# Self-attention: row sums of the exponentials taken from ScalarE's accumulator over the first round's scores, with the layer norm's scaling and the squares given to GpSimd

## The chip, the cores and the metric

The kernel runs on one core of one Trainium2 chip. A core has five engines that run their own instruction streams and wait for each other by semaphores: TensorE (PE, matrix products; its weight loads are listed apart as PEld), VectorE (DVE), ScalarE (ACT), GpSimd (POOL) and SyncE (SP, which here only issues transfers). PE writes to PSUM; the other data lies in SBUF. The metric is the device time of one execution in microseconds (us), lower being better.

## The reference, cut to what matters

The program is one decoder layer in float32 over 32 sequences of 128 tokens with 512 features: differential self-attention, cross-attention, and a mixture of experts. The change touches the self-attention alone:

```python
x = x + attn(layernorm(x))
# in attn: 16 heads with two sides each = 32 score maps of head size 16
q = (x @ Wq) * HD**-0.5 ; k = x @ Wk ; v = x @ Wv       # v: 16 heads of size 32
aw = softmax(q @ k.T + causal)                          # for each head and side
aw = aw[side 0] - lam * aw[side 1]
attn = aw @ v
attn = attn * rsqrt(mean(attn * attn, -1) + 1e-5) * (1 - LAMBDA_INIT)
return attn @ Wo
```

## The kernel before, in words

`self_attention` (from L103) works on the 32 sequences in **steps**. A step (b, cp) handles one sequence b and half of its score maps: CP = 2 chunks c of four heads j, each with two sides, so 16 maps of 128 queries by 128 keys. There are 64 steps, two for each sequence, and the loop from L451 is a software pipeline over them: pass n starts step n and does the later parts of the steps before it.

- `normalize` (L180, by `shifted`, L74): h = x*rstd + down, one ScalarE instruction of 128x512 with two per-partition operands. `turn_in` (L186) transposes h on PE (L83) and copies it out (hT, L194).
- `queries_and_keys` (L196): products L207, one pass for each quarter of the features; ScalarE takes keys and queries out of PSUM (kz, L213; qT, L218); GpSimd makes a second form of the keys, k1 (L214), with one added row that carries the maximum. `values` (L220): product L225, copy L229.
- `maxima` (L231), the first round: the scores go to PSUM with queries as rows (L238); VectorE adds the causal mask and writes them to SBUF as `s` (two instructions, L244), then takes each row's negated maximum into the tile `nm` (two instructions, L251).
- `turn_maxima` (L256), one pass later: nm is transposed on PE (L262) and VectorE puts the maxima into the queries, qm (L264).
- `exponentials` (L270), the second round: the scores are computed again, keys as rows and with the maximum already subtracted (L279); ScalarE takes the exponential of all of them (two instructions of 128x1024, L286); GpSimd sets the masked half to zero in place (two instructions, L289).
- `weigh` (L295), two passes after `maxima`: eight products of v with the exponentials (L303), and eight products of a column of ones with the same exponentials (L309), which give the sums of the softmax. Both land in one PSUM tile `po`, in 32x32 blocks; VectorE transposes the blocks, 128x768, into `u` (L314).
- `divide` (L319): reciprocal of the sums (L323), the second side's times -lambda (L324), and o = u times that (L327).
- `finish` (L334), after a sequence's second step: the two sides are added on GpSimd (at, L338), squared on ScalarE (sq, L342), and summed by head on VectorE (ms, L344 and L345); GpSimd takes the power -1/2 (rr, L347). `scale_out` (L350) multiplies on VectorE (an, L353), `turn_out` transposes (anT, L361), `leave` (L369) multiplies by Wo (L374) and adds the residual (xres, L378).

The steps alternate. I call **step A** the pass that ends a sequence's `weigh` (its `divide` is followed by `finish`) and that holds `values` and `turn_in`; **step B** is the other, with `scale_out` (an) at its head and `leave` (xres) at its end. PSUM is handed out by `bank()` (L48) as four buffers of two banks, in turn: who asks for one waits until the tile of four requests ago has been read. The queries and keys of step A (L207) so wait for the tile that `leave` filled, that is for L378.

A scheduler orders each engine's instructions ahead of time; on the chip every engine works through its list in order. VectorE's list around the change is, in step A: qm, anT, s, nm, then u (L314), L323, L324, o (L327), ms, L345, qm; in step B: an (L353), s, a statistic of the next input (L56), nm, L58, L60, u, L323, L324, o, xres. GpSimd's list is, in step A: k1, two selects (L289), at, rr; in step B: k1, two small layer-norm instructions (L62, L66, of which L62 waits for VectorE's L60), two selects. ScalarE's list is, in step A: kz twice, qT, two exponentials, sq, v, hT, h; in step B: kz twice, qT, two exponentials.

After the self-attention come cross-attention, the shared experts and the routed experts.

Of the kernel before, what the change touches and what calls it, by code (L numbers as in the profile page):

```python
# [10 lines left out]
F32 = mybir.dt.float32  # L11
I32 = mybir.dt.int32
AF = mybir.ActivationFunctionType
ALU = mybir.AluOpType
# [4 lines left out]
P = 128  # L19
# [83 lines left out]
def self_attention(cm, x, x1_d, Wq, Wk, Wv, Wo, lq1, lk1, lq2, lk2, heads, heads_in, beside):  # L103
# [14 lines left out]
    nc, tc, bank = cm.nc, cm.tc, cm.banks  # L118
    B = x.shape[0]
    H, D, G = 16, 32, 2  # L120
    CP = 2
    ROW = (16, 0)
    with ExitStack() as ctx:
        wp = ctx.enter_context(tc.tile_pool(name="a_w", bufs=1))
        p1 = ctx.enter_context(tc.tile_pool(name="a_p1", bufs=1))
        p2 = ctx.enter_context(tc.tile_pool(name="a_p2", bufs=2))
# [6 lines left out]
        xin, xres = {}, {}  # L133
# [37 lines left out]
        nc.scalar.activation(begun, cm.mhalf[:, 0:1], AF.Exp)  # L171

        hT, qT, kz, k1, vs = {}, {}, {}, {}, {}
        h, qm, expd, u, o, an = {}, {}, {}, {}, {}, {}

        def measure(b):
            if b < B:
                h[b] = cm.moments(pj2, xin[b], "a_")

        def normalize(b):  # L180
            if b < B:
                rstd, down = h[b]
                h[b] = pj2.tile([P, E], F32, name="h")
                cm.shifted(h[b], xin.pop(b), rstd, down)

        def turn_in(b):  # L186

# [32 lines left out]
        def values(g, i):  # L220
            if g * G >= B:
                return
            pv = bank()[:, 0, :]
            for ec in range(EC):
                nc.tensor.matmul(  # L225
                    pv, hT[g][:, ec, ts(i, P)], w["wv"][:, ec, :], start=ec == 0, stop=ec == EC - 1
                )
            vs[g, i] = p2.tile([P, E], F32, name="v", bufs=3)
            nc.scalar.copy(vs[g, i], pv)  # L229

        def maxima(b, cp):  # L231

            g, i = divmod(b, G)
            sc = [bank() for _ in range(2)]
            for c in range(CP):
                for j in range(4):
                    rows, oc = ts(j, 32), CP * cp + c
                    nc.tensor.matmul(  # L238
                        sc[j // 2][:, j % 2, ts(c, 2 * P)],
                        qT[g][rows, oc, i, :], kz[g, oc][rows, i], start=True, stop=True,  # L240
                    )
            s = p1.tile([P, 4, CP, 2, P], F32, name="s")
            for pair in range(2):
                nc.vector.tensor_tensor(  # L244
                    s[:, 2 * pair : 2 * pair + 2].rearrange("p j c s k -> p (j c s) k"),
                    sc[pair].rearrange("p j (x k) -> p (j x) k", k=P),
                    causal.unsqueeze(1).broadcast_to([P, 4 * CP, P]), ALU.add,
                )
            for side in range(2):
                at = nm[(CP * b + cp) % 2][:, side].rearrange("p (j r) -> p j r", r=32)  # L250
                nc.vector.tensor_reduce(  # L251
                    at[:, :, ROW[side] : ROW[side] + CP], s[:, :, :, side, :], AX.X, ALU.max,
                    negate=True,
                )

        def turn_maxima(b, cp):  # L256

            g, i = divmod(b, G)
            tr = bank()[:, 0, 0 : 2 * P].rearrange("p (s x) -> p s x", s=2)
            qm[b, cp] = p2.tile([P, 2, CP, P], F32, name="qm")  # L260
            for side in range(2):
                nc.tensor.transpose(tr[:, side], nm[(CP * b + cp) % 2][:, side], cm.ident)  # L262
            for side in range(2):
                nc.vector.scalar_tensor_tensor(  # L264
                    qm[b, cp][:, side], qT[g][:, CP * cp : CP * cp + CP, i, :],
                    others[:, side : side + 1],
                    tr[:, side].unsqueeze(1).broadcast_to([P, CP, P]), ALU.mult, ALU.add,
                )
# [26 lines left out]
        def weigh(b, cp):  # L295


            g, i = divmod(b, G)
            po = bank()
            es = [expd.pop((b, cp, pair)) for pair in range(2)]  # L300
            for c in range(CP):
                for j in range(4):
                    nc.tensor.matmul(  # L303
                        po[ts(j, 32), 0, ts(c, 2 * P)], vs[g, i][:, ts(4 * (CP * cp + c) + j, D)],
                        es[j // 2][:, j % 2, c], start=True, stop=True,
                    )
            for c in range(CP):
                for j in range(4):
                    nc.tensor.matmul(  # L309
                        po[ts(j, 32), 1, 0 : 2 * P], ones[:, c, :], es[j // 2][:, j % 2, c],  # L310
                        start=c == 0, stop=c == CP - 1,
                    )
            u[b, cp] = p1.tile([P, 6, 4, D], F32, name="u")
            nc.vector.transpose(  # L314
                u[b, cp].rearrange("p n k d -> p (n k d)"),
                po.rearrange("p two n -> p (two n)")[:, 0 : 6 * P],
            )

        def divide(b, cp):  # L319

            t = u.pop((b, cp))
            rs = p2.tile([P, CP, 2, 4], F32, name="rs")
            nc.vector.reciprocal(rs.rearrange("p c s k -> p s k c"), t[:, 4:6, :, 0:CP])  # L323
            nc.vector.tensor_scalar(rs[:, :, 1, :], rs[:, :, 1, :], nlam, None, ALU.mult)  # L324
            if cp == 0:
                o[b] = p1.tile([P, 2 * CP, 2, 4 * D], F32, name="o")
            nc.vector.tensor_tensor(  # L327
                o[b][:, CP * cp : CP * cp + CP].rearrange("p c s (k d) -> p (c s k) d", d=D),
                t[:, 0:4].rearrange("p n k d -> p (n k) d"),
                rs.rearrange("p c s k -> p (c s k)").unsqueeze(2).broadcast_to([P, 8 * CP, D]),  # L330
                ALU.mult,
            )

        def finish(b):  # L334

            both = o.pop(b)
            at = p1.tile([P, H, D], F32, name="at")
            nc.gpsimd.tensor_tensor(  # L338
                at.rearrange("p (c k) d -> p c (k d)", c=EC), both[:, :, 0], both[:, :, 1], ALU.add
            )  # L340
            sq = p1.tile([P, H, D], F32, name="sq")
            nc.scalar.activation(sq, at, AF.Square)  # L342
            ms = p2.tile([P, H], F32, name="ms")
            nc.vector.tensor_reduce(ms, sq, AX.X, ALU.add)  # L344
            nc.vector.tensor_scalar(ms, ms, 1.0 / D, EPS, ALU.mult, ALU.add)  # L345
            rr = p2.tile([P, H], F32, name="rr")
            nc.gpsimd.tensor_tensor(rr, ms, cm.mhalf, ALU.pow)  # L347
            an[b] = at, rr
# [48 lines left out]
            )  # L397
        nc.vector.tensor_scalar(others, others, -1.0, 1.0, ALU.mult, ALU.add)


        ones = wp.tile([P, CP, D], F32, name="a_ones")
        nc.vector.memset(ones, 0.0)
        for c in range(CP):
            nc.vector.memset(ones[:, c, c : c + 1], 1.0)

        for b in range(G):
            measure(b)

# [9 lines left out]


        nm = [wp.tile([P, 2, P], F32, name=f"a_nm{i}") for i in range(2)]  # L420
        for t in nm:
            nc.gpsimd.memset(t, 0.0)

        for b in range(G):
            normalize(b)
# [25 lines left out]
        for n in range(len(steps) + 5):  # L451
            g, k = divmod(n, 2 * G)
            if n == len(steps) - 2 * G:
                early.close()
            at = {ago: steps[n - ago] for ago in range(6) if 0 <= n - ago < len(steps)}
            if 1 in at:
                turn_maxima(*at[1])
            if 0 in at:
                maxima(*at[0])
            queries_and_keys(g + 1, k)  # L460
            if 1 in at:
                exponentials(*at[1])
            if 2 in at:
                weigh(*at[2])
            if k % 2:
                values(g + 1, k // 2)
            elif 5 in at:
                leave(at[5][0])
            if 3 in at and at[3][1]:
                scale_out(at[3][0])  # L470
            if 2 in at:
                divide(*at[2])
                if at[2][1]:
                    finish(at[2][0])
            b = (g + 2) * G + k // 2
            if k % 2 == 0:
                measure(b)
                if 4 in at:
                    load_again(at[4][0])
            else:  # L480
                normalize(b)
                turn_in(b)
                load(b + G)
                if 4 in at:
                    turn_out(at[4][0])
            if n in beside:
                beside[n]()


class CrossAttention:  # L490
# [19 lines left out]
    ROW = (16, 0)  # L510
# [612 lines left out]
class Shared:  # L1123
# [4 lines left out]
    G = 4  # L1128
# [540 lines left out]
```

## Time and profile before

| | |
|---|---|
| ten runs | median 3960.17 us (3950.39 to 3965.82) |
| profiled execution | 3958.99 us, its span 3957.3 us |
| granted PE clock, whole run | 0.994 |
| self-attention, even stretch | from 107.13 us to 742.15 us, 25 sequences |
| the same stretch, busy | PE 620.79, PEld 396.45, DVE 494.11, ACT 208.33, POOL 282.53 us of 635.02 |
| self-attention's last product L309 | starts at 848.0 us |

Times in the traces count from the span's start. A line of the timeline gives the start, how long the instruction (or a run of equal instructions, with xN) took, the engine, the line of the code, what it writes and reads, and in brackets how long its engine sat idle before it and what ended that. PE's instructions overlap each other, so that PE's busy share is near the whole wherever it has something in its queue, also when it waits inside. An engine that is idle for part of each sequence is not thereby unimportant: what counts is who waits for it last.

### The profile page before, as it was taken

What the parts mean: (1) busy time and instruction counts of PE and PEld (TensorE: products, weight loads), DVE (VectorE), ACT (ScalarE), POOL (GpSimd) and SP (SyncE); (2) the same over time, 40 slices, a digit from 0 to 9 for tenths busy, and PEclk for the clock granted to TensorE, in tenths of its full rate; (3) what the DMA queues carried; (4) which work ended last, traced back from release to release, by engine and by line L of the source; (5) the groups of instructions that cost most, each with busy time, mean ns of one, the idle gap of its engine ahead of it and who ended that gap; (6) DMA issues with size and microseconds to landing.
All of it is one profiled execution on the core that took longest, in us unless ns stands there. A gap on an engine that the chain in (4) does not pass through costs nothing. (4 is left out here: it accounts for less than half of the span.)

```text
span 3957.3 us, 58171 instructions
## 1 busy us (share of the span) xinstructions
PE 3849.3 (97%) x20020; PEld 2026.3 (51%) x20020; DVE 2200.5 (56%) x3525; ACT 1191.7 (30%) x1696; POOL 2255.8 (57%) x2420
## 2 busy tenths in 40 slices
PE   8999999989999999999999999999999999999999
PEld 5666666633433343434445555555555555555444
DVE  5777777778888888888522333333333333333111
ACT  3333333325655556665410111111111111111000
POOL 4444444453666666666325777777777777775000
PEclk9999999989999999999999999999999999999999
DMA  3101110121111111111126778677777777777210
GB/s 109 33 31 30 33 33 28 33 85 34 57 49 60 49 46 49 49 46 44 41 89 161 182 160 195 142 190 164 176 170 165 170 168 171 167 171 160 80 64 32
DMA packets 285980, 387.22 MB, mean 98 GB/s; under 512 B 147888, under 2 KB 179248, under 8 KB 285616
## 3 DMA queue, kind: packets, MB, share of 16 engines
q0 software_dynamic: 62912, 109.85, 15.9%
q1 hardware_dynamic: 81792, 190.98, 15.2%
q10 hardware_dynamic: 140976, 82.60, 7.5%
q8 instruction: 162, 2.65, 0.3%
q14 instruction: 138, 1.13, 0.1%
HBM read 617.52 MB, written 143.07 MB: 192 GB/s over the span
## 5 line engine op out<-in xcount | busy, mean ns | idle before, releaser
L1381 POOL DMA_INDIRECT e_xr<-h_d,e_run_of x832 | 849.4, 1021 | 288.4 <-issue 267.9
L653 DVE TENSOR_REDUCE nm<-ps 128x2 f32<-128x1024 f32 x512 | 610.8, 1219 | 61.6 <-PE ps L649 59.9
L1411 DVE TENSOR_TENSOR e_gu<-e_act,ps 128x352 f32<-128x352 f32 x208 | 108.4, 521 | 930.6 <-ACT e_act L1410 930.6
L676 ACT ACTIVATE xp<-ps 128x1024 f32<-128x1024 f32 x512 | 510.3, 1022 | 282.3 <-PE ps L649 213.7
L1442 PE MATMUL ps<-wd,e_guT 128*128 128x512 f32 (+1 forms) x1248 | 570.1, 592 | 2.0 <-issue 2.0
L672 PE MATMUL ps<-xqn,xk 32*128 32x512 f32 x2048 | 537.8, 623 | 20.2 <-ACT xp L676 19.8
L649 PE MATMUL ps<-xk,xq 32*128 32x512 f32 x2048 | 537.2, 628 | 1.5 <-DVE xres L378 1.4
L1406 PE MATMUL ps<-wg,e_xT 128*128 128x352 f32 x1664 | 528.2, 460 | 4.8 <-DMA wg<-in_L_ffn_w_gate_dram 4.8
L1406 PE MATMUL ps<-wu,e_xT 128*128 128x352 f32 x1664 | 526.6, 459 | 0.9 <-DMA wu<-in_L_ffn_w_up_dram 0.9
L1406 PEld LDWEIGHTS ps<-wg,e_xT 128*128 128x128 f32 x1664 | 315.2, 190 | 239.6 <-issue 104.2
L1406 PEld LDWEIGHTS ps<-wu,e_xT 128*128 128x128 f32 x1664 | 315.8, 190 | 178.4 <-DMA wu<-in_L_ffn_w_up_dram 3.1
L1447 POOL DMA_INDIRECT sum_d<-e_y,e_into x208 | 338.2, 1626 | 117.1 <-issue 69.5
L1442 PEld LDWEIGHTS ps<-wd,e_guT 128*128 128x128 f32 (+1 forms) x1248 | 237.2, 190 | 246.6 <-issue 203.8
L1410 ACT ACTIVATE e_act<-ps 128x352 f32<-128x352 f32 x208 | 96.4, 463 | 886.5 <-PE ps L1406 832.4
L672 PEld LDWEIGHTS ps<-xqn,xk 32*128 32x128 f32 x2048 | 165.2, 183 | 243.2 <-ACT xp L676 101.0
L1446 ACT ACTIVATE e_y<-ps,e_weight 128x512 f32<-128x512 f32 x208 | 142.9, 687 | 422.6 <-PE ps L1442 415.3
L1432 DVE STREAM_TRANSPOSE e_guT<-e_gr 96x384 f32<-96x384 f32 (+1 forms) x416 | 230.4, 554 | 63.9 <-DMA e_gr<-e_gu_d 57.4
L687 PE MATMUL ps<-xp,v 128*32 128x512 f32 x2048 | 246.0, 598 | 8.8 <-ACT xp L676 8.7
L987 POOL DMA_INDIRECT table_d<-entry,at x192 | 196.5, 1023 | 71.8 <-issue 48.0
L1393 DVE STREAM_TRANSPOSE e_xT<-e_xr 128x512 f32<-128x512 f32 x208 | 226.1, 1087 | 11.9 <-DMA e_xr<-h_d,e_run_of 11.9
L214 POOL TENSOR_SCALAR k<-kz,a_keep,a_extra 128x256 f32<-128x256 f32 x128 | 70.0, 556 | 259.0 <-ACT kz L213 259.0
L649 PEld LDWEIGHTS ps<-xk,xq 32*128 32x128 f32 x2048 | 161.2, 183 | 31.0 <-issue 9.4
(267 smaller groups left out, 4956.2 us busy)
## 6 DMA issues: line engine op xcount, KB each, us to landing
wg<-in_L_ffn_w_gate_dram SPq DMA_DIRECT2D x208, 704.0 KB
wu<-in_L_ffn_w_up_dram SPq DMA_DIRECT2D x208, 704.0 KB
wd<-in_L_ffn_w_down_dram SPq DMA_DIRECT2D x208, 576.0 KB
e_gu_d<-e_gu ACTq DMA_DIRECT2D x208, 192.0 KB
e_gr<-e_gu_d ACTq DMA_DIRECT2D x208, 192.0 KB
wd<-in_L_ffn_w_down_dram SPq DMA_DIRECT2D x208, 128.0 KB
e_xr<-h_d,e_run_of POOLq DMA_INDIRECT x832, 3.4
xres<-in_x_dram SPq DMA_DIRECT2D x32, 256.0 KB
```

Of the source, the lines that this page charges most:

```text
L649: self.nc.tensor.matmul(sc[:, i, :], q[rows, ts(c, P)], k[rows, :], start=True, stop=True)
L653: self.nc.vector.tensor_reduce(at[:, self.ROW[side], 2 * pair : 2 * pair + 2], sc, AX.X, ALU.max, negate=True)
L672: self.nc.tensor.matmul(sc[:, i, :], k[rows, ts(c, P)], q[rows, :], start=True, stop=True)
L676: self.nc.scalar.activation(e, sc, AF.Exp)
L687: self.nc.tensor.matmul(po[b, side][ts(j, 32), :], self.v2[b % 2][:, c, 2 * j + side, :], es[j // 2][:, j % 2, :], start=c == 0, stop=c == ...
L987: self.nc.gpsimd.indirect_dma_start(out=self.table_ds[k % 2][:, :], out_offset=bass.IndirectOffsetOnAxis(ap=self.at[b][:, k : k + 1], axis=0),
L1381: self.cm.nc.gpsimd.indirect_dma_start(out=xr[:, t, :], out_offset=None, in_=self.h3_d.rearrange("t (q f) -> (t q) f", q=self.Q), in_offse ...
L1393: self.cm.nc.vector.transpose(xT.rearrange("p c (t i) -> p c t i", t=self.Q), self.xr.pop(i).rearrange("p t (j c) -> p c t j", c=EC),)
L1406: nc.tensor.matmul(pgu[:, half, 0:M], t[:, c, :], w[:, c, :], start=c == 0, stop=c == EC - 1)
L1432: self.cm.nc.vector.transpose(t[rows, 0:n, :].rearrange("p c (t i) -> p c t i", t=self.Q), g[rows, :, 0 : 32 * n].rearrange("p t (j c) -> ...
L1442: nc.tensor.matmul(py, t[:n, c, :], self.wd[s][:n, c, :], start=c == 0, stop=c == len(M_CHUNKS) - 1)
L1447: nc.gpsimd.indirect_dma_start(out=self.sum_d[:, :], out_offset=bass.IndirectOffsetOnAxis(ap=self.into[:, i : i + 1], axis=0), in_=y[:, :] ...
```

## The change

The sums of the softmax come from the first round's scores: `sums` takes the exponential of each of the 16 maps of `s` (128x128) on ScalarE, with the row's negated maximum as bias, and lets ScalarE's accumulator put the row's sum into one column of a new tile `sm`. It works in place on `s`, which therefore has two buffers and not one. In `weigh` the eight products with ones are gone; one PE transpose of `sm` takes their place, `u` has 128x640 elements and not 128x768, and `divide` reads the sums from their new places. Two pieces of ScalarE's work go to GpSimd: the layer norm's scaling from the fifth sequence on, and the squares.

```diff
     def normalize(b):
...
-                cm.shifted(h[b], xin.pop(b), rstd, down)
+                if b < 2 * G:
+                    cm.shifted(h[b], xin.pop(b), rstd, down)
+                else:
+                    nc.gpsimd.tensor_scalar(h[b], xin.pop(b), rstd, down, ALU.mult, ALU.add)
...
-            s = p1.tile([P, 4, CP, 2, P], F32, name="s")
+            s = sc_of[b, cp] = p2.tile([P, 4, CP, 2, P], F32, name="s")
...
+        def sums(b, cp, c):
+            n = (CP * b + cp) % 2
+            s = sc_of[b, cp]
+            for j in range(4):
+                for side in range(2):
+                    at = 32 * j + ROW[side] + c
+                    to = 32 * j + 2 * c + side
+                    nc.scalar.activation(
+                        s[:, j, c, side, :], s[:, j, c, side, :], AF.Exp,
+                        bias=nm[n][:, side, at : at + 1], accum_out=sm[n][:, to : to + 1],
+                    )
...
-            for c in range(CP):
-                for j in range(4):
-                    nc.tensor.matmul(
-                        po[ts(j, 32), 1, 0 : 2 * P], ones[:, c, :], es[j // 2][:, j % 2, c],
-                        start=c == 0, stop=c == CP - 1,
-                    )
-            u[b, cp] = p1.tile([P, 6, 4, D], F32, name="u")
+            nc.tensor.transpose(po[:, 1, 0:P], sm[(CP * b + cp) % 2], cm.ident)
+            u[b, cp] = p1.tile([P, 5, 4, D], F32, name="u")
             nc.vector.transpose(
                 u[b, cp].rearrange("p n k d -> p (n k d)"),
-                po.rearrange("p two n -> p (two n)")[:, 0 : 6 * P],
+                po.rearrange("p two n -> p (two n)")[:, 0 : 5 * P],
             )
...
-            nc.vector.reciprocal(rs.rearrange("p c s k -> p s k c"), t[:, 4:6, :, 0:CP])
+            nc.vector.reciprocal(rs.rearrange("p c s k -> p k (c s)"), t[:, 4, :, 0 : 2 * CP])
...
-            nc.scalar.activation(sq, at, AF.Square)
+            nc.gpsimd.tensor_tensor(sq, at, at, ALU.mult)
...
             if 1 in at:
                 turn_maxima(*at[1])
+                sums(*at[1], 0)
             if 0 in at:
                 maxima(*at[0])
             queries_and_keys(g + 1, k)
             if 1 in at:
                 exponentials(*at[1])
+                sums(*at[1], 1)
```

As the scheduler places it, VectorE's list keeps its order. ScalarE's list is now, in step A: kz twice, qT, two exponentials, nine sums, v, hT, seven sums; in step B: kz twice, qT, two exponentials, sixteen sums. The sixteen sums in step B read the `s` that step A wrote, and the next step A writes into that same buffer; likewise the sums in step A read the `s` of the step B before. GpSimd's list is, in step A: k1, two selects, at, sq, h, rr. From cross-attention on, every engine's list is what it was.

More of the change, by code (lines that the diff above doesn't have):

```diff
@@ L173, in self_attention @@
         hT, qT, kz, k1, vs = {}, {}, {}, {}, {}
-        h, qm, expd, u, o, an = {}, {}, {}, {}, {}, {}
+        h, sc_of, qm, expd, u, o, an = {}, {}, {}, {}, {}, {}, {}
         def measure(b):
@@ L254, in maxima @@
                 )
+        def sums(b, cp, c):
[9 more added lines that the diff above has]
+                    )
+            if c == CP - 1:
+                del sc_of[b, cp]
         def turn_maxima(b, cp):
@@ L398, in self_attention @@
         nc.vector.tensor_scalar(others, others, -1.0, 1.0, ALU.mult, ALU.add)
[L401 to L404, printed above, removed]
         for b in range(G):
@@ L420, in self_attention @@
         nm = [wp.tile([P, 2, P], F32, name=f"a_nm{i}") for i in range(2)]
-        for t in nm:
+        sm = [wp.tile([P, P], F32, name=f"a_sm{i}") for i in range(2)]
+        for t in nm + sm:
             nc.gpsimd.memset(t, 0.0)
```

## The prediction, made before the changed kernel was run

> **What bounds the kernel now.** I read the page first, then the busy times of one stage, then two steps of the timeline, engine by engine. The page points at PE:
>
> ```profile
> PE 3849.3 (97%) x20020; PEld 2026.3 (51%) x20020; DVE 2200.5 (56%) x3525; ACT 1191.7 (30%) x1696; POOL 2255.8 (57%) x2420
> ```
>
> That is a mean over stages. The change touches only self-attention, so here is that stage, 100 us of it:
>
> ```profile
> core 0: us, PE busy (x) PEld busy (x) DVE busy (x) ACT busy (x) POOL busy (x), PEclk, DMA share, GB/s
> 400.00:500.00 100.00, 97.94 (x860) 62.21 (x858) 78.41 (x110) 33.56 (x56) 45.57 (x48) 1.00 0.11 31
> ```
>
> By these shares PE is full, and ScalarE has 66 us in 100 to give away. But the weight loads fill only 62%, so PE's busy time hides waits. The timeline of one sequence (step A from 449.44 us, step B from about 462 us) tells who waits for whom:
>
> ```profile
> 454.36 1.94 ACT L286 ACTIVATE e<-ps 128x1024 f32<-128x1024 f32 x2
> 455.14 1.05 PE L309 MATMUL ps<-e,a_ones 128*32 128x256 f32 x16
> 455.46 2.13 POOL L289 TENSOR_SCALAR_AFFINE_SELECT e<-e 128x1024 f32<-128x1024 f32 x2 [0.53 <-ACT e L286]
> 456.26 0.98 DVE L314 STREAM_TRANSPOSE u<-ps 128x768 f32<-128x768 f32 x1 [0.78 <-PE ps L309]
> 457.57 0.23 DVE L324 TENSOR_SCALAR rs<-rs,nlam 128x8 f32<-128x8 f32 x1
> 457.83 0.69 DVE L327 TENSOR_TENSOR o<-u,rs 128x512 f32<-128x512 f32 x1
> 458.61 1.27 POOL L338 TENSOR_TENSOR at<-o 128x512 f32<-128x512 f32 x1 [1.02 <-DVE o L327]
> 459.91 0.63 ACT L342 ACTIVATE sq<-at 128x512 f32<-128x512 f32 x1 [3.61 <-POOL at L338]
> 460.57 0.69 DVE L344 TENSOR_REDUCE ms<-sq 128x16 f32<-128x512 f32 x1 [2.04 <-ACT sq L342]
> 461.55 2.92 POOL L347 TENSOR_TENSOR rr<-ms,mhalf 128x16 f32<-128x16 f32 x1 [1.67 <-DVE ms L345]
> 464.50 0.69 DVE L353 SCALAR_TENSOR_TENSOR an<-at,rr 128x512 f32<-128x512 f32 x1 [2.26 <-POOL rr L347]
> 465.11 2.35 DVE L244 TENSOR_TENSOR s<-ps,causal 128x1024 f32<-128x1024 f32 x2
> ...
> 467.40 1.94 ACT L286 ACTIVATE e<-ps 128x1024 f32<-128x1024 f32 x2 [0.40 <-PE ps L279]
> 470.43 0.15 DVE L60 TENSOR_SCALAR a_ln_ve<-a_ln_mv 128x1 f32<-128x1 f32 x1
> 471.31 0.26 POOL L66 TENSOR_SCALAR a_ln_down<-a_ln_mv,a_ln_rstd 128x1 f32<-128x1 f32 x1
> 471.52 2.14 POOL L289 TENSOR_SCALAR_AFFINE_SELECT e<-e 128x1024 f32<-128x1024 f32 x2
> 471.80 0.84 DVE L324 TENSOR_SCALAR rs<-rs,nlam 128x8 f32<-128x8 f32 x1
> 472.67 1.53 DVE L327 TENSOR_TENSOR o<-u,rs 128x512 f32<-128x512 f32 x1
> 474.12 0.68 DVE L378 TENSOR_TENSOR xres<-xres,ps 128x512 f32<-128x512 f32 x1
> 474.85 1.59 PEld L207 LDWEIGHTS ps<-hT,wk 128*128 128x128 f32 x8 [0.79 <-DVE xres L378]
> ```
>
> Read it as a loop, each line starting where the one before it ends. PE's L309 ends at 456.19 and u starts. Then o, at, sq, ms, rr, an and s follow with gaps under 0.1 us. In step B the masked scores lead on to xres, and PE's next L207 waits for xres to free its PSUM buffer: the loop closes, 25.36 us after 449.49. Its parts: from xres to u 6.82 us (PE: L207, L279, L303, L309); u to the end of o 2.26; o to s 6.59; s to the end of xres 9.69 (465.11 to 474.80). VectorE alone, without PE's part, is only 0.78 us shorter: that is how long u waits for L309. So a saving counts only on this loop, and PE's share in it is one L309 of the two in a sequence.
>
> One more thing is to be seen: L324 takes 0.84 us in step B and 0.23 in step A; o takes 1.53 and 0.69. In step B two selects run on GpSimd, each 1.09 us (471.52 to 472.61, to 473.66). L324 ends at 472.64, just behind the first; o ends 0.54 us behind the second. These two instructions make no headway while a select runs. In step A the selects end at 457.59, as L324 starts.
>
> **The change part by part,** in the times of this lap.
>
> *L309 out, a transpose in (step A).* L303's last product ends at 455.33 (16 in 1.07 us from 454.26). A PE transpose of 128x128 takes 0.27 us (the L262 rows, weight load 0.14 us); u follows 0.07 us behind as now, so near 455.71: 0.55 us earlier, with bounds of 0.4 and 0.7 for how soon the transpose can start. VectorE is free from 455.48.
>
> *u is smaller.* 768 elements take 0.98 us, 512 (L361) 0.70: one 128 less is 0.14 us less, 0.84. L324 would start at 456.87 and o end at 457.82, 0.70 earlier than now. But the selects still run until 457.59, since they hang on step A's exponentials, which do not move. If L324 waits as in step B, it ends at 457.62 and o at 458.34. **The gain is then 0.18 us and not 0.70.** The Trainium skill ("SBUF — State Buffer", section "Who interferes with whom") states that GpSimd and such a VectorE instruction exclude each other for a whole instruction, whichever starts first; step B's rows show it, no row shows it in step A. By it the lap gains 0.18 here, without it 0.70.
>
> *u in step B* gains nothing: o's end there hangs on the selects, and they on L60, L62 and L66, which stay.
>
> *Squares on GpSimd.* A 128x512 product of two SBUF operands there is L338's row, 1.27 us, for 0.63 plus a hop of 0.03 on ScalarE: **0.61 us more on the loop**. ScalarE's v copy, which stood behind sq, may come 0.6 us sooner, but off the loop.
>
> *Normalization on GpSimd* stands between sq and rr. The nearest row is GpSimd's L626, a tensor_scalar of 128x512 with two per-partition operands, 0.77 us median. rr waits for ms and L345 anyway (0.92 us from the end of sq), so h costs 0 to 0.1; I take 0. Behind it wait only rr and k1. Its reader, PE's transposes, comes a sequence later, so that wait is covered, as is the input's load behind it.
>
> Lap so far: 25.36 - 0.18 + 0.61 = 25.79 us, 0.43 more; over 32 sequences 14 us. If L324 isn't held: 25.36 - 0.70 + 0.61 = 25.27, 3 us less in all.
>
> *Sixteen sums a step on ScalarE.* No row shows an accumulator. The nearest rows give what one costs without it:
>
> ```profile
> L213 ACT ACTIVATE kz<-ps,a_keep 128x256 f32<-128x256 f32 x128 | 53.6, 470 | 389.4 <-PE ps L207 389.4
> L218 ACT ACTIVATE qT<-ps 128x256 f32<-128x256 f32 x64 | 24.5, 383 | 0.0
> ```
>
> L218 against the 1.02 us of 128x1024 (L286) makes 0.83 ns an element; the square of 128x512 from SBUF takes 0.63, so 128 elements 0.31. A per-partition operand adds 0.09 (L213 against L218): 0.40. Two L213 in a row take 0.84, not 0.94: 0.10 of each overlaps. At least 0.30 each, then. The sum must be written to another tile after the last element. If that is free, 0.30; if it is like an instruction of its own, the one-element rows say 0.20 (L171 0.202, L440 0.211): with no overlap 0.60. I take 0.40 + 0.20 - 0.10 = **0.50 us each**, since only the start of the next sum can overlap, and keep 0.30 and 0.60.
>
> The Trainium skill ("ScalarE: Activation LUTs", section "What ACT_TABLE_LOAD costs") gives 280 ns and 0.833 ns an element for an ACTIVATE with a pointer as bias, with 93 ns overlap in a row: an estimate of 0.29 us for each sum, and it prices no accumulator; by it the sums would be hidden and the lap 25.79. No run here shows it yet.
>
> At 0.50 the step's sums take 8.0 us. In step B they stand behind the exponentials (end 469.34), 16 in a row; kz waits behind them until 478.6, so nothing else is late. But they read the s of step A, and the next step A's s (476.13) overwrites that buffer: a new wait on VectorE, with nm, and then u, queued behind it. That makes a second loop: s in B to the end of B's exponentials 4.23 us, sixteen sums, s and nm of A 4.70, u to o 2.13 (0.84 and the unheld rows), o to s in B 6.59 + 0.61 = 7.20. Together 18.26 us and sixteen sums. It equals 25.79 at 0.47 us a sum. At 0.50 it is 26.26, **0.90 us more than now**; at 0.60 it is 27.86, 2.50 more. In step A nine sums stand ahead of v: 456.30 + 4.5 = 460.8, for 460.44 now, and all end near 465.5, about when B's s wants that buffer (465.11 + 0.5): no further cost at 0.50. ScalarE's total, some 7 us + 32 x 0.50 = 23 us in a lap of 26, still fits.
>
> **The sum.** 25 laps were counted from 107.13 to 742.15 us; the first and last sequences, which run less regularly, are charged alike. 32 x 0.90 = 29 us on the profiled 3958.99: 3988 us. The ten runs' median, 3960.17, is 1.2 us above that; I leave it.
>
> **The rivals.**
>
> 1. *Sums heavier, 0.60 us:* 32 x 2.50 = 80, so 4039 us. For it: sixteen short instructions in a row with nothing between them. Against: the rows overlap. 18%.
> 2. *Sums hidden (0.47 or less):* the port wait and GpSimd's square are left, 14 us, 3973 us. For it: 0.30 is what the rows give without the accumulator. 22%.
> 3. *L324 isn't held and the sums are hidden:* 3 us less, 3956 us, no change to be told. The u gain pays for the square. 14%.
> 4. *Faster, because PE decides:* if PE's stream, and not VectorE's loop, sets the pace, each step loses L309's slot (455.14 to 456.12, 0.98 us) and gets a transpose with its load (0.38): 64 x 0.60 = 38 us less, 3921 us. This needs the loop to have slack of 0.6 us that the brackets above do not show, and sums under 0.47. 8%.
>
> That the sums work as drawn but another wait (v behind nine sums) holds PE is in rival 1's price.
>
> **The numbers.** My forecast, 3988 us, has 38%. About 0.2%, 8 us, is what a measurement of this kernel can tell from no change. Slower by more: forecast, rivals 1 and 2, 78%; same: rival 3, 14%; faster: rival 4, 8%. The range, 3953 to 4041 us, takes in 0.30 to 0.60 us a sum with and without the held L324, and leaves out rival 4 and what lies above rival 1.
>
> **What would show it.** Right: s of step A (or B) waits for the sums on ScalarE; the step between two an (L353) is near 26.3 us; the sums stand 0.5 us apart; L324 in step A is longer than 0.23; sq on GpSimd 1.27 and ms behind it. Wrong: VectorE's s never waits for ScalarE (rival 2 or 3), L324 keeps 0.23 in step A (3), u no longer waits on anything of VectorE's and PE's L207 not for xres (4). What would upset all of it: a readout of the accumulator far from 0 to 0.2 us.

## The result, and the profile after

| | before | after |
|---|---|---|
| median of the comparison | 3961.14 us (28 runs) | 3977.26 us (8 runs) |
| ratio after/before | | 1.0044, 95% interval 1.0035 to 1.0053 |
| profiled execution, span | 3958.99, 3957.3 us | 3978.24, 3976.2 us |
| distance of two `an`, most laps | 25.36 us | 25.76 us |
| first `an` / last `an` | 83.92 / 861.82 us | 92.20 / 878.08 us |
| granted PE clock, whole run | 0.994 | 0.990 |

The change makes the kernel 0.44% slower. The forecast (3988 us) has the sign and is 11 us too high; rival 2 of the prediction (3973 us) is 4 us too low and nearer. The forecast's mechanism, a wait of VectorE for the sums, was wrong, as the traces show. Line numbers from here on are those of the changed kernel: L210 was L207, s is L247, nm L254, the sums L268, the selects L308, u L328, the product with -lambda L338 (it was L324), o L341, at L352, sq L356, h L187, an L367, xres L392.

The same 100 us window of the self-attention, in the columns shown before. PE has lost its products with ones and not gained in pace: its share is 91% where it was 98%. ScalarE's went from 34% to 75%.

```profile
core 0: us, PE busy (x) PEld busy (x) DVE busy (x) ACT busy (x) POOL busy (x), PEclk, DMA share, GB/s
400.00:500.00 100.00, 91.16 (x724) 57.23 (x722) 80.47 (x108) 74.71 (x289) 49.67 (x55) 0.98 0.10 31
```

One lap of the changed kernel, from the timeline (step B from 453.16 us, step A from 463.58):

```profile
453.16 0.69 DVE L367 SCALAR_TENSOR_TENSOR an<-at,rr 128x512 f32<-128x512 f32 x1 [2.26 <-POOL rr L361]
453.77 2.35 DVE L247 TENSOR_TENSOR s<-ps,causal 128x1024 f32<-128x1024 f32 x2
...
456.64 2.33 DVE L254 TENSOR_REDUCE a_nm<-s 128x8 f32<-128x1024 f32 x2
...
460.25 2.14 POOL L308 TENSOR_SCALAR_AFFINE_SELECT e<-e 128x1024 f32<-128x1024 f32 x2
460.32 1.04 DVE L338 TENSOR_SCALAR rs<-rs,nlam 128x8 f32<-128x8 f32 x1
461.40 1.53 DVE L341 TENSOR_TENSOR o<-u,rs 128x512 f32<-128x512 f32 x1
462.85 0.67 DVE L392 TENSOR_TENSOR xres<-xres,ps 128x512 f32<-128x512 f32 x1
463.58 1.99 PE L210 MATMUL ps<-hT,wk 128*128 128x256 f32 x8 [1.25 <-DVE xres L392]
...
469.60 2.13 POOL L308 TENSOR_SCALAR_AFFINE_SELECT e<-e 128x1024 f32<-128x1024 f32 x2 [0.59 <-ACT e L305]
469.70 0.85 DVE L328 STREAM_TRANSPOSE u<-ps 128x640 f32<-128x640 f32 x1
...
470.87 0.88 DVE L338 TENSOR_SCALAR rs<-rs,nlam 128x8 f32<-128x8 f32 x1
471.79 0.69 DVE L341 TENSOR_TENSOR o<-u,rs 128x512 f32<-128x512 f32 x1
472.57 1.27 POOL L352 TENSOR_TENSOR at<-o 128x512 f32<-128x512 f32 x1 [0.84 <-DVE o L341]
473.91 1.04 POOL L356 TENSOR_TENSOR sq<-at 128x512 f32<-128x512 f32 x1
474.94 0.77 POOL L187 TENSOR_SCALAR h<-xin,a_ln_rstd,a_ln_down 128x512 f32<-128x512 f32 x1
474.99 0.69 DVE L358 TENSOR_REDUCE ms<-sq 128x16 f32<-128x512 f32 x1 [2.50 <-POOL sq L356]
475.97 2.92 POOL L361 TENSOR_TENSOR rr<-ms,mhalf 128x16 f32<-128x16 f32 x1 [0.26 <-DVE ms L359]
478.92 0.69 DVE L367 SCALAR_TENSOR_TENSOR an<-at,rr 128x512 f32<-128x512 f32 x1 [2.26 <-POOL rr L361]
```

It is the loop of the prediction: xres frees PE's L210, PE leads to u, and o, at, sq, ms, rr, an and s follow on each other. Its parts, before and after: end of xres to u 6.82 and 6.18; u to the end of o 2.26 and 2.78; o to s 6.59 and 7.05; s to the end of xres 9.69 and 9.75. Together 25.36 and 25.76. In step A, L338 now stands 0.88 us and not 0.23, until 471.75: the selects, which start at 469.60, end at 471.73. No s waits for ScalarE: of its 128 instructions two wait at all, for PE's scores.

The sums by the groups (count, busy time and mean ns of one, idle time before): each is two instructions, an ACTIVATE and a readout of the accumulator.

```profile
L268 ACT ACTIVATE s<-s,a_nm 128x128 f32<-128x128 f32 x1024 | 396.4, 393 | 25.2 <-DVE a_nm L254 21.5 <-PE ps L326 3.2
L268 ACT ACTIVATION_READ_ACCUMULATOR s<-s,a_nm 128x1 f32 x1024 | 197.0, 192 | 0.0
```

In a row, on ScalarE's timeline, behind the exponentials of step B:

```profile
457.95 0.40 ACT L268 ACTIVATE s<-s,a_nm 128x128 f32<-128x128 f32 x1
458.26 0.19 ACT L268 ACTIVATION_READ_ACCUMULATOR s<-s,a_nm 128x1 f32 x1
459.00 0.40 ACT L268 ACTIVATE s<-s,a_nm 128x128 f32<-128x128 f32 x1 [0.55 <-DVE a_nm L254]
459.31 0.19 ACT L268 ACTIVATION_READ_ACCUMULATOR s<-s,a_nm 128x1 f32 x1
459.40 0.39 ACT L268 ACTIVATE s<-s,a_nm 128x128 f32<-128x128 f32 x1
...
459.78 0.39 ACT L268 ACTIVATE s<-s,a_nm 128x128 f32<-128x128 f32 x1
...
467.34 0.84 ACT L216 ACTIVATE kz<-ps,a_keep 128x256 f32<-128x256 f32 x2 [2.46 <-PE ps L210]
```

Three things are to be seen. The starts lie 0.39 us apart, not 0.50: both the next ACTIVATE and the readout begin some 0.1 us before what stands ahead of them ends. The second sum, the first that needs the other side's maxima, waits for the second of the two instructions of this same step B's nm (L254, 456.64 to 458.97): the sixteen sums of step B read step B's own s. The description of the change and the prediction had them read that of step A, which is wrong; by the order of ScalarE's list the sums of step A then read step A's own s too. And behind the sixteen ScalarE stands idle for 2.46 us until PE's next keys.

Ahead of the even stretch the first `an` is already 8.3 us late. The first scores, kernel before:

```profile
41.58 2.36 DVE L244 TENSOR_TENSOR s<-ps,causal 128x1024 f32<-128x1024 f32 x2 [7.22 <-PE ps L238]
44.72 0.69 DVE L56 BATCH_NORM_STATS2 a_ln_stats<-xin 128x6 f32<-128x512 f32 x1 [0.78 <-DMA xin<-in_x_dram]
46.68 0.30 PE L262 MATMUL ps<-ident,a_nm 128*128 128x128 f32 x1 [1.48 <-DVE a_nm L251]
46.91 0.71 PE L238 MATMUL ps<-kz,qT 32*128 32x256 f32 x6
```

and after:

```profile
42.54 0.69 DVE L56 BATCH_NORM_STATS2 a_ln_stats<-xin 128x6 f32<-128x512 f32 x1 [9.64 <-DMA xin<-in_x_dram]
43.15 2.34 DVE L247 TENSOR_TENSOR s<-ps,causal 128x1024 f32<-128x1024 f32 x2
47.42 0.45 PE L281 MATMUL ps<-ident,a_nm 128*128 128x128 f32 x1 [3.68 <-DVE a_nm L254]
47.80 1.23 PE L241 MATMUL ps<-kz,qT 32*128 32x256 f32 x6
...
65.43 1.13 PE L241 MATMUL ps<-kz,qT 32*128 32x256 f32 x12 [1.68 <-ACT v L232]
66.49 3.33 PE L210 MATMUL ps<-hT,wk 128*128 128x256 f32 x8
```

L56, a statistic of a later input, has slipped ahead of the first s in VectorE's list and waits for that input's transfer; so VectorE's list does not keep its order in the first sequences, as the description of the change says it does. PE waits 3.68 us for the maxima where it waited 1.48, and then again 1.68 us for v, which stands behind sums on ScalarE; behind each wait its products are slow (six of L241 in 1.23 us for 0.71, L210 in 3.33 us where a lap shows 1.99). Between 40 and 70 us the granted clock is 0.78, before 0.94. The Trainium skill ("TensorE: Matmul & The Clock Gate", section "What's actually happening") has the clock fall after about 3.4 us without work; the 3.68 us agree, but the slow L210 behind a wait of 1.68 us is not explained by that alone, nor is a like group of 3.40 us in the kernel before, which stands behind the wait of 1.48 us.

### The profile page after: what moved, and what is told of

Read it like the earlier page. It is cut to its first block, busy times and chain, and to the rows that moved or that the text cites. A ratio compares the mean times of both kernels' runs of the same rounds, so it can differ in the third digit from the quotient of the medians.

```text
span 3976.2 us, 58556 instructions
## 1 busy us (share of the span) xinstructions
PE 3815.7 (96%) x19060; PEld 1999.1 (50%) x19060; DVE 2217.4 (56%) x3522; ACT 1549.2 (39%) x3684; POOL 2311.6 (58%) x2482
## 5 line engine op out<-in xcount | busy, mean ns | idle before, releaser
L268 ACT ACTIVATE s<-s,a_nm 128x128 f32<-128x128 f32 x1024 | 396.4, 393 | 25.2 <-DVE a_nm L254 21.5
```

Source lines behind the costliest of these rows:

```text
L268: nc.scalar.activation(s[:, j, c, side, :], s[:, j, c, side, :], AF.Exp, bias=nm[n][:, side, at : at + 1], accum_out=sm[n][:, to : to + 1],)
```

## The experiments

The theory after the result: the sums are hidden in the even stretch, and the lap is longer by the square on GpSimd less what the held L338 leaves of u's gain; the rest is the late start. The rival is the prediction's: the sums hold VectorE. Each ratio is against runs of the kernel before on the same chip, with its 95% interval.

### The parts of the change, each alone

**sq_pool**, the kernel before with the squares on GpSimd:

```diff
-            nc.scalar.activation(sq, at, AF.Square)
+            nc.gpsimd.tensor_tensor(sq, at, at, ALU.mult)
```

> The kernel before with one part of the change alone: the squares go from ScalarE to GpSimd. My theory (the loop from xres over u, o, at, sq, ms, rr, an and s back to xres sets the pace): in the trace after, sq takes 1.04 us on GpSimd and starts 0.07 us behind at, against 0.63 and 0.03 on ScalarE, so the loop is 0.45 us longer: the distance between two an goes from 25.36 to 25.8 us, the time up by about 14 us, to 3975. Rival (PE sets the pace, the loop has slack): distance 25.36, no change; as ScalarE's v copy comes sooner, perhaps 25.0 and 10 us less.

Measured: ratio 1.0042 (1.0029 to 1.0055), lap 25.81 us, first `an` at 83.71. One line of the change, without any sum, costs as much as the whole change.

```profile
467.76 1.04 POOL L342 TENSOR_TENSOR sq<-at 128x512 f32<-128x512 f32 x1
```

**sums_only**, the changed kernel with squares and h back on ScalarE:

```diff
-                if b < 2 * G:
-                    cm.shifted(h[b], xin.pop(b), rstd, down)
-                else:
-                    nc.gpsimd.tensor_scalar(h[b], xin.pop(b), rstd, down, ALU.mult, ALU.add)
+                cm.shifted(h[b], xin.pop(b), rstd, down)
...
-            nc.gpsimd.tensor_tensor(sq, at, at, ALU.mult)
+            nc.scalar.activation(sq, at, AF.Square)
```

> The changed kernel with the squares and the normalization back on ScalarE: the sums by the accumulator alone. ScalarE's list in step A is then two exponentials, seven sums, sq, v, hT, nine sums, h. My theory: seven sums of 0.386 us end at about 459.0, before at is ready at 459.7, so sq is not late; u comes 0.6 us sooner but L324 waits for the selects, so the loop gains 0.18 us: distance of two an 25.2 us; the lead-in keeps its 9 us (the first sums stand ahead of the first exponentials): 3963 to 3966 us. Rival A (the sums on ScalarE hold the loop): distance over 25.4, time above 3972. Rival B (PE sets the pace): distance near 24, time near 3930.

Measured: ratio 1.0019 (1.0009 to 1.0028), lap 25.70: a miss by 0.5 us. The sums did not hold the square, which starts 0.03 us behind at. The scheduler had laid VectorE's list otherwise. In step A half of qm now stands between the two instructions of ms, so rr starts 0.26 us later; in step B L56 stands behind nm, so the selects, o and xres come 0.26 later. 25.20 and these two make 25.72. So this run shows the sums in another order of VectorE's list than the changed kernel's, not in that one.

```profile
472.17 0.69 DVE L355 TENSOR_REDUCE ms<-sq 128x16 f32<-128x512 f32 x1 [2.05 <-ACT sq L353]
472.78 0.47 DVE L280 SCALAR_TENSOR_TENSOR qm<-qT,a_others,ps 128x256 f32<-128x256 f32 x1
473.17 0.17 DVE L356 TENSOR_SCALAR ms<-ms 128x16 f32<-128x16 f32 x1
```

First `an` 87.75, 3.8 us later than before, with L56 in its old place: that is the sums' own share of the late start.

**h_pool**, the kernel before with h on GpSimd from the fifth sequence on (the expectation says ninth, by mistake):

```diff
-                cm.shifted(h[b], xin.pop(b), rstd, down)
+                if b < 2 * G:
+                    cm.shifted(h[b], xin.pop(b), rstd, down)
+                else:
+                    nc.gpsimd.tensor_scalar(h[b], xin.pop(b), rstd, down, ALU.mult, ALU.add)
```

> The kernel before with one part of the change alone: from the ninth sequence on h is computed on GpSimd. Theory: in the even stretch it costs nothing (lap 25.36 to 25.4 us, before 25.36); but the scheduler now places L56, a statistic of an input that is still arriving, ahead of the first s in VectorE's list, so PE waits some 3.5 us for the first maxima where it waited 1.5, its granted clock falls, and the first an comes at 87 to 88 us and not at 83.9. Time 3 to 5 us longer than before, ratio 1.0008 to 1.0013. Rival (h stands between sq and rr on GpSimd and holds rr): lap 25.8 to 26.1, ratio 1.003 to 1.005.

Measured: ratio 1.0013 (1.0002 to 1.0025), lap 25.43, first `an` 86.12. L56 does slip ahead of s:

```profile
42.63 0.69 DVE L56 BATCH_NORM_STATS2 a_ln_stats<-xin 128x6 f32<-128x512 f32 x1 [9.32 <-DMA xin<-in_x_dram]
43.24 2.34 DVE L247 TENSOR_TENSOR s<-ps,causal 128x1024 f32<-128x1024 f32 x2
```

The late start by it is 2.2 us, less than expected, and the lap costs 0.07 us, so the rival that rr is held falls. In step B GpSimd's L62 starts 0.15 us behind L60 for 0.09, and the selects, o and xres come later by that; why it does is not shown. The edit acts from the fifth sequence on and still moves the first, through the scheduler's order.

The three parts do not add up to the whole: their laps grow by 0.45, 0.34 and 0.07 us, 0.86 together, and the whole change's by 0.40. Without the 0.52 us of the other order of VectorE's list in sums_only the three make 0.34.

**sq_vector**, the changed kernel with the squares on VectorE:

```diff
-            nc.gpsimd.tensor_tensor(sq, at, at, ALU.mult)
+            nc.vector.tensor_tensor(sq, at, at, ALU.mult)
```

> The changed kernel with the squares on VectorE, so that h, the sums and the transposes stay as changed. Theory: on VectorE the square takes 0.69 us behind at and ms follows it at once, 0.4 to 0.5 us less than GpSimd's 1.04 and its hops; the lap falls from 25.76 to 25.3 us, the ratio to 1.0010 to 1.0020. Rival (the changed kernel's longer lap has another cause, the sums or h): lap stays at 25.7 or more and the ratio at 1.004.

Measured: ratio 1.0013 (1.0004 to 1.0022), lap 25.37, the lap of the kernel before to 0.01 us.

**after_again**, the changed kernel unaltered, on the chip of sq_vector and h_pool.

> The changed kernel unaltered, timed on the same chip as its variants of this batch. Both theories: lap 25.76 us, first an near 92 us, ratio 1.0035 to 1.0053.

Measured: ratio 1.0044 (1.0031 to 1.0056), lap 25.77, first `an` 91.64. On one chip, then, moving the squares from GpSimd to VectorE takes away 0.31% of the change's 0.44%.

### Are the sums hidden, and by how much?

The next three, and late_vec further down, ran on a chip where the kernel before took 4008 us; only their ratios and laps are compared with the others.

**sums_24** takes eight sums of step B twice, into columns that nobody reads:

```diff
+            if c == 1 and cp == 0:
+                for j in range(4):
+                    for side in range(2):
+                        at, to = 32 * j + ROW[side], 32 * j + 4 + side
+                        nc.scalar.activation(
+                            s[:, j, 0, side, :], s[:, j, 0, side, :], AF.Exp,
+                            bias=nm[n][:, side, at : at + 1], accum_out=sm[n][:, to : to + 1],
+                        )
```

> The changed kernel, but step B issues twenty-four sums in a row and not sixteen: the eight of one chunk are taken a second time, into columns of sm that nobody reads. Step A keeps its sixteen, and every other engine's list is the same. Theory (the prediction's second loop, with the price measured in the profile after, 0.386 us a sum): step A's s then has to wait for the sums on ScalarE, the lap is 18.26 + 24 x 0.386 = 27.5 us and the time 1.75 us x 22 to 32 laps longer than the changed kernel's 3977, 4015 to 4033 us. Rival (ScalarE, with some 22 us of work in a lap of 25.8, has room, and nobody waits for the sums): the lap stays at 25.8 and the time at 3977.

Measured: ratio 1.0096 (1.0068 to 1.0124), lap 25.88 us. The second loop of the prediction, whose lap was 27.5 us, does not exist. The lines of VectorE and ScalarE (L276 are the added sums; u is L336, the product with -lambda L346, o L349):

```profile
474.71 2.31 DVE L247 TENSOR_TENSOR s<-ps,causal 128x1024 f32<-128x1024 f32 x2
...
480.73 0.23 DVE L346 TENSOR_SCALAR rs<-rs,nlam 128x8 f32<-128x8 f32 x1
481.00 1.46 DVE L349 TENSOR_TENSOR o<-u,rs 128x512 f32<-128x512 f32 x1
```

```profile
477.34 0.39 ACT L276 ACTIVATE s<-s,a_nm 128x128 f32<-128x128 f32 x1
477.72 0.81 ACT L216 ACTIVATE kz<-ps,a_keep 128x256 f32<-128x256 f32 x2
```

Step A's s starts at 474.71 with no wait, while step B's sums run until 477.7: they read another buffer. (One s in the whole run, at 316.58, is listed as waiting 0.88 us for L276; but it starts before the last L276, 316.45 to 316.84, has ended, and behind PE's scores, which end at 316.48.) What the eight do is use up ScalarE's 2.46 us of idle time: 8 x 0.386 = 3.1 us. Counted from PE's L210, the keys of step A come 0.5 us later than in the changed kernel, the exponentials and selects 0.3 us, and now the selects hold o (1.46 us) and not L346 (0.23). That is the 0.12 us of the lap. The total grew by more than the lap explains (22 x 0.12 = 3 us): the last `an` comes at 895.85, 13.9 us behind after_again's on its other chip, through the start (first `an` 94.67, and 2.7 us in the next two laps), one lap of 31.29 us around 300 us for 29.89, and 4 us in the last eight.

**no_sums** leaves the sums out; sm holds a constant, so the softmax is not normalized:

```diff
-        for t in nm + sm:
+        for t in nm:
             nc.gpsimd.memset(t, 0.0)
+        for t in sm:
+            nc.gpsimd.memset(t, 16.0)
...
-                sums(*at[1], 0)
...
-                sums(*at[1], 1)
```

> The changed kernel without its 1024 sums; the tile of the sums holds a constant, so the softmax is left unnormalized. Theory: in the even stretch the sums are hidden, so the lap stays at 25.76 us; in the first 90 us they stand ahead of keys, queries and exponentials in ScalarE's list, so the first an (92.2 us in the changed kernel, 83.9 in the kernel before) comes 4 to 9 us earlier and the time is 3968 to 3973 us. Rival (the sums slow the even stretch too, by what they read from SBUF while others do): the lap falls to 25.4 to 25.6 and the time to 3955 to 3963. Rival (the late start comes from GpSimd's list): first an still near 92 and the time near 3977.

Measured: lap 25.75 to 26.07 us (median 25.86), first `an` 87.51, as the theory has it; but the ratio is 1.0054 (1.0038 to 1.0070), no gain over the change. The last `an` comes at 882.00, as in after_again (881.98): every second or third lap is 0.1 to 0.3 us longer than 25.75, at a granted clock of 0.96 in the stretch for 0.99. So the usual lap does not get shorter without the sums, and the whole does not confirm that taking them away gives anything back. The products saw other numbers here, and the chip was another; what lowered the clock stays open.

**no_select** leaves out the two selects, so the masked exponentials stay in the second product:

```diff
-                nc.gpsimd.affine_select(
-                    out=flat, in_=flat, compare_op=ALU.is_ge, fill=0.0, base=0,
-                    pattern=[[0, 4 * CP], [1, P]], channel_multiplier=-1,
-                )
```

> The changed kernel without the two selects of each step on GpSimd, so the exponentials above the diagonal stay in the second product. Theory (the product with -lambda and o make no headway while a select runs): the product with -lambda takes 0.23 us in both steps, for 0.88 in step A and 1.04 in step B now, and o 0.69 in step B for 1.53; both held times go, and the lap falls to between 22.8 (PE's own pace) and 23.9 us, the time to 3905 to 3930. Rival (the two are long because of what they read, after the transpose of u): 0.88 and 1.04 us stay, and the lap shortens only by the selects' place ahead of the v products.

Measured: 3983.74 us in one run, lap 23.70. The lap is as expected; the time is above the expected one, on a chip where the kernel before took 4008 us in the median. The two instructions in step B (L334 and L337 here), which took 1.04 and 1.53 us:

```profile
477.75 0.23 DVE L334 TENSOR_SCALAR rs<-rs,nlam 128x8 f32<-128x8 f32 x1
478.01 0.69 DVE L337 TENSOR_TENSOR o<-u,rs 128x512 f32<-128x512 f32 x1
```

In step A they take 0.23 and 0.69 as well. So the selects made them long. The Trainium skill's rule ("SBUF — State Buffer", section "Who interferes with whom") holds here in both steps.

### Taking the loop apart

**late_before** and **late_after** issue `an` behind step B's o in VectorE's list, in the kernel before and in the changed one; s no longer waits for rr:

```diff
+        last = [None]
...
-            nc.vector.tensor_tensor(
+            last[0] = nc.vector.tensor_tensor(
                 o[b][:, CP * cp : CP * cp + CP].rearrange("p c s (k d) -> p (c s k) d", d=D),
...
-            if 3 in at and at[3][1]:
-                scale_out(at[3][0])
...
                 if at[2][1]:
                     finish(at[2][0])
+            if 3 in at and at[3][1]:
+                with tc.issue_after(last[0].ins):
+                    scale_out(at[3][0])
```

> The kernel before with one edit in VectorE's order: an (scale_out) is issued behind step B's o and no longer ahead of step B's s, so VectorE doesn't wait for rr at that place. The same work, the same results. My theory: the loop loses the wait for rr and becomes 6.82 + 2.26 + 3.65 + 10.30 = 23.0 us, so that PE's own stream binds next, which I put at 24.2 us (25.35 less the waits of 0.36, 0.30 and 0.39 us that its rows show): distance of two an 24.2, some 35 us less, 3925 us. Rival (PE sets the pace already): no change, 25.36.

> The changed kernel with the same edit: an behind step B's o. My theory: the loop becomes 6.18 + 2.78 + 4.10 + 10.36 = 23.4 us and PE's stream, without the products with ones, 24.2 - 2 x 0.70 = 22.8: distance of two an 23.4, some 75 us less than the changed kernel, near 3903 us, and less than late_before by 20 us or more: the change is then worth its PE time. Rival A (the sums on ScalarE hold it): distance stays above 25.4. Rival B (PE sets the pace): only what PE lost, no difference from the changed kernel.

Measured: late_before 0.9921 (0.9905 to 0.9936), lap 24.15 (23.8 to 24.5); late_after 0.9851 (0.9831 to 0.9872), lap 23.42. One lap of late_before:

```profile
352.72 0.68 DVE L354 SCALAR_TENSOR_TENSOR an<-at,rr 128x512 f32<-128x512 f32 x1
...
376.87 0.68 DVE L354 SCALAR_TENSOR_TENSOR an<-at,rr 128x512 f32<-128x512 f32 x1
```

and one of late_after:

```profile
380.39 0.68 DVE L368 SCALAR_TENSOR_TENSOR an<-at,rr 128x512 f32<-128x512 f32 x1
...
403.81 0.68 DVE L368 SCALAR_TENSOR_TENSOR an<-at,rr 128x512 f32<-128x512 f32 x1
```

In these laps VectorE no longer sits idle ahead of `an`, where it waited 2.26 us for rr. The loop is what bounded both kernels, and once s is out of it the change is a gain: it lies 0.7% under the same edit without it by the ratios, 0.6% by the medians (3910.55 and 3933.80 us, on one chip).

**late_vec** is late_after with at and sq on VectorE:

```diff
-            nc.gpsimd.tensor_tensor(
+            nc.vector.tensor_tensor(
                 at.rearrange("p (c k) d -> p c (k d)", c=EC), both[:, :, 0], both[:, :, 1], ALU.add
             )
...
-            nc.gpsimd.tensor_tensor(sq, at, at, ALU.mult)
+            nc.vector.tensor_tensor(sq, at, at, ALU.mult)
```

> The changed kernel with an issued behind step B's o on VectorE, and with at and sq on VectorE instead of GpSimd. Theory: VectorE's loop then asks for 22.3 us a lap, less than PE's own stream (22.8), so PE decides: lap 22.8 us, time 3885 to 3895 us. Rival (VectorE becomes the bound by its own queue: two more instructions of 0.69 us and the locks of GpSimd's selects on them): lap 23.4 us or more, no gain over the same edit without the move, 3910 us.

Measured: 0.9816 (0.9784 to 0.9847), lap 22.64: faster than both kernels. The same 100 us show PE without a gap:

```profile
core 0: us, PE busy (x) PEld busy (x) DVE busy (x) ACT busy (x) POOL busy (x), PEclk, DMA share, GB/s
400.00:500.00 100.00, 99.88 (x816) 63.36 (x811) 93.88 (x134) 86.84 (x342) 51.01 (x54) 1.00 0.12 36
```

**late_vec_h** is late_vec with h back on ScalarE, by the first hunk of sums_only.

> The kernel with an behind step B's o and with at and sq on VectorE, and now with h back on ScalarE for all sequences. Theory: PE sets the pace still, lap 22.64 us; the first s stands ahead of L56 again, so the first sequence is 3 to 4 us earlier: ratio 0.9805 to 0.981, for 0.9816 with h on GpSimd. Rival (ScalarE, busy 85% of the stretch already, now holds keys and queries back in step A): lap 22.8 to 23.4 us and a ratio of 0.983 or more.

Measured: 0.9845 (0.9832 to 0.9858), lap some 23.3: the rival's size, by another way than it named. h now stands behind seven sums on ScalarE, and starts 4.2 us after sq (in late_vec 0.4); so the input's buffer comes free later, and L56 waits for the next input (between 320 and 700 us 13 times, 8.8 us in all):

```profile
464.46 0.69 DVE L56 BATCH_NORM_STATS2 a_ln_stats<-xin 128x6 f32<-128x512 f32 x1 [0.65 <-DMA xin<-in_x_dram]
```

u, the selects (by L60 and L62) and xres come behind L56, and PE's products then wait for xres, 13 times too and 8.7 us in all, for which no product waits there in late_vec. By the laps h on GpSimd pays 0.7 us at this pace; in the kernel before it cost 0.07 us (h_pool). The two ratios, taken on two chips, do not settle it: their intervals meet.

## Why the prediction was right and where it failed

- **The loop was right.** It closes over the same instructions after the change, and taking s out of it (late_before) shortens the lap by 1.2 us where PE's share of 98% said that nothing was to be had.
- **The transpose in place of L309, and the smaller u:** predicted 0.55 us earlier and 0.84 us long, measured 0.64 and 0.85.
- **The held L338 in step A was right:** 0.88 us, ending with the selects, and only 0.12 us of the gain is left at the end of o (0.18 predicted).
- **The square was over-priced:** its row was at's, 1.27 us, and it took 1.04; o to s grew by 0.46 and not by 0.61. Without the sums the predicted lap was 25.79; measured is 25.76.
- **h at no cost was nearly right:** 0.07 us a lap in h_pool, within the 0 to 0.1 given. Its effect on the order at the start was not seen.
- **The failed step is the second loop,** "the next step A's s (476.13) overwrites that buffer". Step B's sums read step B's own s, which is written again only a lap later. sums_24 shows it: sums worth 16 x 0.58 us in step B cost 0.12 us a lap, where 18.26 + 16p, with p the price of a sum, gave 1.76. So the forecast's 26.26 us would not have come at 0.50 us a sum either; its term for the laps was 29 us, and they grew by 8.0 us over all (878.08 - 92.20, less 861.82 - 83.92). By the rows of the changed kernel the cover was ScalarE's 2.46 us of idle time behind the sixteen: an estimate from them is that a sum stays hidden up to about 0.386 + 2.46/16 = 0.54 us.
- **The price of a sum was too high as well:** 0.386 us for 0.50. The step "only the start of the next sum can overlap" was wrong, since in the rows the readout overlaps too, by 0.1 us. The two errors went the same way. What happened in the stretch is rival 2, which was given 22%: its lap to 0.03 us.
- **The start was not priced.** The forecast charged the first sequences like all others; they cost 8.3 us to the first `an`, as much as all laps together. Of it the sums alone show 3.8 us (sums_only), the reordering by h 2.2 (h_pool), the square nothing (sq_pool, 83.71); what makes the two together more than 6.0 was not separated. The 16 us by which the last `an` is late, and 2.6 us behind it, are the 18.9 us of span. That 3977 us fell near 3988 was luck: the start and the end that were left out (8.3 and 2.6 us) and the loop that was put in wrongly (32 x 0.47 = 15 us) are of like size.

## What to carry to other kernels

Before pricing a wait on a buffer, find in the order of the instructions which tile each group reads: whether a sum belongs to this step or the last one decided here whether it could hold anything. Where a chain over several engines closes on itself, a change is worth only what it does on that chain, whatever the busy shares say; one square on it cost four times (0.46 us) what 16 products less in each sequence had freed there (0.12, with the product with -lambda held by the selects), and opening the chain first turned the same change into a gain. Price the lead-in by itself: a scheduler may reorder it for an edit that starts to act many passes later.

## What the runs showed of the hardware

- An ACTIVATE with an accumulator is two instructions, 0.393 and 0.192 us for 128 elements, and in a row one such pair takes 0.386 us: both of its parts overlap with what precedes them.
- On GpSimd the product of a 128x512 tile with itself took 1.04 us, the sum of two halves of another tile into one of that size 1.27.
- A granted clock of 0.78 between 40 and 70 us, for 0.94, behind two waits of 3.68 and 1.68 us: eight products of 128x256 took 3.3 to 3.8 us instead of 1.99 (the kernel before shows one such group, 3.40 us at 49.26).
